# Two registers for the row bound of all indirect gathers, set once, in a sparse four-layer graph kernel

## The chip, the cores and the metric

The kernel runs on one core of a Trainium2 chip. The metric is device time in microseconds for the whole launch, as the median of several runs. Lower is better.

## What is computed

Four graph layers follow each other on the same node features and the same adjacency matrix: 8 batches, 2048 nodes, 128 features. The adjacency matrix is random, symmetric, with about 17 neighbours for each node. Layers 0 and 2 are attention with 8 heads of 16, masked by the adjacency, followed by a feed-forward part:

```python
scores = jnp.einsum('bnhd,bmhd->bhnm', Q, K) / jnp.sqrt(HEAD_DIM)
scores = jnp.where(mask, -jnp.inf, scores)
attn = jax.nn.softmax(scores, axis=-1)
attn_out = jnp.einsum('bhnm,bmhd->bnhd', attn, V).reshape(B, N, OUT_DIM)
x = _layer_norm(h + (attn_out @ Wo + bo), ln1_g, ln1_b)
y = jax.nn.relu(x @ W1 + b1) @ W2 + b2
x = _layer_norm(x + y, ln2_g, ln2_b)
```

Layers 1 and 3 are graph attention with one score for each edge:

```python
h = x @ W
e = (h @ a_src)[:, :, None] + (h @ a_dst)[:, None, :]
e = jnp.where(e >= 0, e, NEG_SLOPE * e)
att = jax.nn.softmax(jnp.where(adj[None] == 0, -jnp.inf, e), axis=-1)
y = jnp.einsum('bij,bjd->bid', att, h) + x          # then a layer norm
```

## The kernel before

The kernel works on the edges that exist and not on the full 2048 x 2048 matrix. It first reads the adjacency matrix in 16 blocks of 128 rows and makes, for each of 32 units of 64 nodes, a list of neighbour indices: the tile `idx`, 128 partitions by 32 units by 9 columns (`TILES`), so 9 columns of 128 edge slots for each unit and, as two groups of 32 nodes share a step, 5 steps (`TG`) for each unit. Beside the lists it makes matrices of ones and zeros (`hot`, kept in DRAM as `hots`) that spread a node's query to its edge slots and add the slots' results up again on TensorE (PE).

A layer first has a table in DRAM with one row for each node, made by the layer before (`project`, L1533 and L1535; the rows leave SBUF through `trows`). For attention a row holds keys and values of all 8 batches (2048 f32), for graph attention 1040 f32. Then for each unit and step `gather` (L1654 and after) issues one or two indirect DMAs on GpSimd (POOL): each reads one column of `idx` and fetches 128 rows of the table into a buffer `kv`, of which there are six. 9 such DMAs for each unit, 32 units and 4 layers make 1152.

An attention step then goes: PE spreads the queries (`qe`, L1734), VectorE (DVE) multiplies them with the gathered keys (L1746) and sums each head (L1753), ScalarE (ACT) takes the exponential (L1763), POOL multiplies it into the values (L1772; DVE does it for some steps), and PE adds the slots up (L1804). A graph attention step has DVE add and fold the scores (L1970, L1977, L1992), ACT the exponential (L1982), and PE add up (L2008). After the five steps of a unit follow the normalizations, the feed-forward part and the rows of the next table.

The order of all this is made before the launch: every piece of work has a key and estimated costs, a planner (`Plan.order`) simulates the engines with these and writes one fixed order for each engine. So each engine takes its instructions strictly in that order. POOL's queue holds, in the layers, almost only two kinds of work: the gathers (L1671) and the multiplications (L1772). Ahead of both stand semaphore waits where the order of the engines needs them.

An indirect DMA is given a bound for its row index. Rows above it are left out without an error (`oob_is_err=False`); the empty edge slots of a list use that. The bound is `nodes - 1`, where `nodes` is 2048, or 1920 for the first steps of the first four units, which read a table whose last rows are still missing: 128 of the 1152 gathers. The DMA instruction takes the bound from a register of POOL. With `bounds_check` given as a number, the language puts a register move ahead of each gather, on POOL's queue.

Where the profile names POOLq, it is POOL's sequencer, which takes the instructions in order, performs moves and semaphore waits itself and hands the rest to the engine.

Of the kernel before, what the change touches and what calls it, by code (L numbers as in the profile page):

```python
# [20 lines left out]
P = 128  # L21
# [50 lines left out]
class Dense:  # L72
# [10 lines left out]
    def __init__(self, ctx, tc, x, adj, w, out):  # L83
        self.tc, self.nc, self.w, self.x_in, self.out = tc, tc.nc, w, x, out
        self.B, self.N, _ = x.shape
        self.NB = self.N // P
        self.NC = self.N // CH

        def pool(name, **kw):
            return ctx.enter_context(tc.tile_pool(name=name, **kw))  # L90

        self.const = pool("const", bufs=1)
        self.dram = pool("dram", bufs=1, space=DRAM)
        self.dram2 = pool("dram2", bufs=2, space=DRAM)
        self.ps_s = pool("ps_s", bufs=2, space=PSUM)
        self.ps_acc = pool("ps_acc", bufs=1, space=PSUM)
        self.ps_m = pool("ps_m", bufs=1, space=PSUM)

        self.constants()
        self.layers = [  # L100
            self.mha_weights(n) if kind is MHA else self.gat_weights(n)
            for n, kind in enumerate(LAYERS)
        ]
        self.masks(adj)

        self.one = pool("one", bufs=1)
        self.two = pool("two", bufs=2)
        self.three = pool("three", bufs=3)
        self.four = pool("four", bufs=4)
        self.kpool = pool("kpool", bufs=9)  # L110
        self.vpool = pool("vpool", bufs=5)
        self.turn = 0
# [656 lines left out]
class Sparse:  # L769
# [15 lines left out]
    def __init__(self, ctx, tc, x, xt, xk, adj, w, out):  # L785
        self.tc, self.nc, self.w, self.xt_in, self.xk_in, self.out = tc, tc.nc, w, xt, xk, out
        self.B, self.N, _ = x.shape
        self.NB = self.N // P
        self.NU = self.N // UNIT
        self.HB = self.B // 2  # L790

        def pool(name, **kw):
            return ctx.enter_context(tc.tile_pool(name=name, **kw))

        self.nc.scalar.preload_act_table_set("natural_log_exp_and_others")
        self.const = pool("const", bufs=1)
        self.dram = pool("dram", bufs=1, space=DRAM)
        self.plan = Plan(self.nc)
        self.op, self.cell = self.plan.op, self.plan.cell
        for tag, bufs in SBUF_BUFS.items():  # L800
            self.plan.pool(tag, pool(f"sb_{tag}", bufs=bufs), bufs, tag in BY_KEY)
        for tag, bufs in PSUM_BUFS.items():
            self.plan.pool(tag, pool(f"ps_{tag}", bufs=bufs, space=PSUM), bufs)

        self.constants()
        self.weights_at = [Cell() for _ in LAYERS]
        self.keys_at = Cell()
        self.late = self.tight = False
        self.whole()
        self.gates = {}  # L810

        self.gate = self.keys_at
        keys = self.const.tile([P, 2 * P], F32, name="Wkv_0")
        self.fill(0, (keys[:, 0:P], w[0]["Wk"]), (keys[:, P : 2 * P], w[0]["Wv"]), at=self.keys_at)
        self.layers = [{"Wkv": keys}]


        self.tables = [
            self.dram.tile([self.N, self.B * (2 * P if kind is MHA else P + 2)], F32, name=f"table_{n}")
            for n, kind in enumerate(LAYERS)  # L820
        ]
        self.table = [Cell() for _ in LAYERS]
        self.rest = [Cell() for _ in LAYERS]

        self.xd = self.dram.tile([self.NU, P, CH], F32, name="xd")
        self.x_at = [Cell() for _ in range(self.NU)]
        self.hots = self.dram.tile([self.NU, P, HOT], F8, name="hots")
        self.hots_at = [Cell() for _ in range(self.NU)]
        self.kept = {}
        self.ends_at = [None] * self.NU  # L830
        self.t = self.const.tile([P, self.NU, P // GROUP * self.HB], F32, name="t")
        self.t_at = [Cell() for _ in range(self.NU)]
        self.idx = self.const.tile([P, self.NU, TILES], I32, name="idx")
        self.idx_at = [Cell() for _ in range(self.NU)]


        self.owner = self.const.tile([P, self.NU, TG, 2], F32, name="owner")
        self.ends = self.const.tile([P, self.NU, 2], F32, name="ends")
        self.late_ends = self.const.tile([P, LATE, 2], F32, name="late_ends")
        self.shift = self.const.tile([P, LATE, 2], F16, name="shift")  # L840

        self.empty = self.const.tile([P, self.NU, TILES], F32, name="empty")


        self.seen = self.const.tile([P, 4, self.NB], F32, name="seen")
        self.stats = self.const.tile([P, 6], F32, name="stats")
        self.eps = self.fixed("eps", EPS)
        self.half = self.fixed("half", 0.5)
        self.rows_n = self.fixed("rows_n", float(self.N))
        self.huge = self.fixed("huge", 1e30)  # L850

# [590 lines left out]
    def rows(self, tag, shape, axis, unit, name=None):  # L1444

        if self.made is None:
            return self.cell(tag, shape, name=name)
        if self.taken == len(self.made):
            self.made.append(self.cell(tag, shape, name=name))
        cut = (slice(None),) * axis + (slice(self.blocks.start * unit, self.blocks.stop * unit),)  # L1450
        self.taken += 1
        return Part(self.made[self.taken - 1], lambda t: t[cut])
# [210 lines left out]
    def gather(self, n, u, t, width, key, kv, rows, writes, shares=()):  # L1663

        tiles = 1 if t == TG - 1 else 2
        nodes = self.N - P if u < LATE and t < PAIRS else self.N

        def start(e):
            for j in range(tiles):
                col = 2 * t + j  # L1670
                e.indirect_dma_start(  # L1671
                    out=rows(kv.tile, j),
                    out_offset=None,
                    in_=self.tables[n][0:nodes],
                    in_offset=bass.IndirectOffsetOnAxis(ap=self.idx[:, u, col : col + 1], axis=0),
                    bounds_check=nodes - 1,
                    oob_is_err=False,
                )

        self.op(  # L1680
            {"POOL": 1.3 * tiles},
            start,
            key,
            reads=[*self.sources(n, u, t), self.idx_at[u]],
            writes=writes,
            shares=shares,
            port="wait",
            dma=120 * tiles * width * 4,
        )
# [539 lines left out]
```

## Time and profile before

| what | value |
|---|---|
| median of 3 runs | 2952.3 us (2948.37, 2952.3, 2961.27) |
| the profiled execution, its own time | 2960.0 us |
| its span, first to last instruction | 2958.3 us |
| granted TensorE clock, mean over the span | 0.893 |
| PE, DVE, ACT, POOL busy | 77%, 78%, 48%, 72% |
| DMA traffic | 1022.52 MB, 346 GB/s on average |

The profile is of one execution. "Busy" is the share of the span in which an engine's own work ran; instructions that a sequencer performs itself, such as register moves and waits, are not in it. A group's row gives the line, the engine, the operation, what it writes and reads, how often, its total and mean time, and how long the engine stood idle just ahead of it, with what ended most of that idle time; "issue" is idle time that the profile can put down to no wait. The row of slices under DMA gives the busy share of the DMA engines in tenths, for 40 equal parts of the span.

### The profile page before, as it was taken

The numbers are of one execution on the slowest core, as the hardware profiler recorded it, in microseconds if no ns is written. First come the engines' busy times: TensorE is split into PE (matmuls) and PEld (weight loads), VectorE is DVE, ScalarE is ACT, GpSimd is POOL, SyncE is SP. The second block draws the span as 40 slices with busy tenths as digits, with TensorE's granted clock in tenths as the row PEclk, the third lists the DMA queues.
The fourth block names the chain that finished last, engine by engine and source line by source line (L and its number), as shares of the span: only waits on it lengthen the run. The fifth ranks groups of instructions, "written<-read, shape, count | busy, mean of one in ns | idle before, by whom it ended". The sixth has DMA issues, their size and how long they took to land. (4 is left out here: it accounts for less than half of the span.)

```text
span 2958.3 us, 59482 instructions
## 1 busy us (share of the span) xinstructions
PE 2282.4 (77%) x21668; PEld 1334.4 (45%) x21668; DVE 2305.8 (78%) x3785; ACT 1423.9 (48%) x4899; POOL 2137.4 (72%) x1455
## 2 busy tenths in 40 slices
PE   6567778777887777778877688888888888777775
PEld 4423333333333334666665243343433333566664
DVE  7789999898977787555554888888898898576665
ACT  5535555555544443555554244444444444354443
POOL 1287778778878775666663788778887786677774
PEclk8778989989989999889898799999999999887787
DMA  8788889889879887999998898988998997899996
GB/s 302 274 315 333 336 324 341 320 330 369 332 299 353 313 308 267 362 410 410 405 406 325 321 380 333 376 339 347 368 374 338 357 370 278 328 404 407 404 398 268
DMA packets 248062, 1022.52 MB, mean 346 GB/s; under 512 B 39184, under 2 KB 52880, under 8 KB 175856
## 3 DMA queue, kind: packets, MB, share of 16 engines
q0 software_dynamic: 166464, 864.44, 75.4%
q1 hardware_dynamic: 81296, 154.18, 14.1%
q8 instruction: 174, 2.85, 0.4%
q14 instruction: 128, 1.05, 0.1%
HBM read 978.23 MB, written 88.08 MB: 360 GB/s over the span
## 5 line engine op out<-in xcount | busy, mean ns | idle before, releaser
L1671 POOL DMA_INDIRECT kv<-table,idx x1152 | 1199.7, 1041 | 583.2 <-issue 324.7
L1772 POOL TENSOR_TENSOR kv<-kv 128x2048 f32<-128x2048 f32 (+1 forms) x259 | 924.6, 3581 | 95.5 <-ACT kv L1763 91.2
L1746 DVE TENSOR_TENSOR kv<-qe,kv 128x2048 f32<-128x2048 f32 (+1 forms) x320 | 662.2, 2069 | 120.6 <-DMA kv<-table,idx 65.1
L1753 DVE TENSOR_REDUCE s<-kv 128x128 f32<-128x2048 f32 (+1 forms) x320 | 659.6, 2061 | 9.9
L1734 PE MATMUL qe<-q_sb,hot 32*128 32x512 f32 (+1 forms) x2304 | 398.2, 697 | 180.4 <-DVE kv L1746 176.6
L1804 PE MATMUL acc<-kv,hot 128*32 128x512 f32 (+1 forms) x2304 | 370.8, 654 | 71.8 <-POOL kv L1772 44.5
L2008 PE MATMUL acc_q<-kv,w 128*32 128x129 f32 (+1 forms) x4608 | 206.8, 311 | 119.6 <-DVE w L1992 98.7
L1992 DVE TENSOR_TENSOR w<-hot,e 128x512 f32<-128x512 f32 (+1 forms) x384 | 221.4, 598 | 53.2 <-ACT e L1982 37.3
L1763 ACT ACTIVATE kv<-s 128x128 f32<-128x128 f32 (+1 forms) x320 | 95.3, 298 | 347.6 <-DVE s L1753 222.7
L1734 PEld LDWEIGHTS qe<-q_sb,hot 32*128 32x128 f32 (+1 forms) x2304 | 106.8, 197 | 310.3 <-DVE kv L1746 251.4
L2008 PEld LDWEIGHTS acc_q<-kv,w 128*32 128x32 f32 (+1 forms) x4608 | 162.6, 128 | 149.7 <-DVE w L1992 110.6
L1970 DVE TENSOR_TENSOR e<-te,kv 128x16 f32<-128x16 f32 (+1 forms) x320 | 58.5, 183 | 195.7 <-DMA kv<-table,idx 194.5
L1607 ACT ACTIVATE junk<-ps_c 128x128 f32<-128x128 f32 x494 | 136.6, 277 | 137.8 <-PE ps_c L1495 117.3
L1471 ACT COPY trows<-ps_p 128x512 f32<-128x512 f32 (+1 forms) x238 | 112.8, 475 | 178.2 <-PE ps_p L1535 100.0
L1804 PEld LDWEIGHTS sums<-kv,hot 128*32 128x32 f32 (+1 forms) x2304 | 90.6, 120 | 212.0 <-issue 206.9
L1495 PE MATMUL ps_c<-centre,r 128*128 128x128 f32 x1024 | 153.7, 298 | 31.6 <-DVE r L1881 17.3
L1505 PE MATMUL ps_f<-x,W 128*128 128x512 f32 (+1 forms) x264 | 153.2, 666 | 29.0 <-ACT hidden L1901 21.7
L1982 ACT ACTIVATE e<-e 128x16 f32<-128x16 f32 (+1 forms) x320 | 65.0, 212 | 228.5 <-DVE e L1977 221.2
L1495 PEld LDWEIGHTS ps_c<-centre,r 128*128 128x128 f32 x1024 | 133.1, 203 | 73.1 <-DVE r L1881 32.2
L1804 PEld LDWEIGHTS acc<-kv,hot 128*32 128x32 f32 (+1 forms) x2304 | 55.9, 115 | 217.5 <-POOL kv L1772 107.6
L1911 PE MATMUL ps_y<-hidden,W 128*128 128x512 f32 (+1 forms) x264 | 146.6, 644 | 8.6 <-ACT hidden L1901 7.3
L1640 ACT ACTIVATE normed<-ps_c,rstd 128x128 f32<-128x128 f32 x495 | 143.2, 370 | 5.7 <-DVE normed L1642 3.8
(204 smaller groups left out, 3850.7 us busy)
## 6 DMA issues: line engine op xcount, KB each, us to landing
x<-xd SPq DMA_DIRECT2D x96, 256.0 KB
xd<-xnew SPq DMA_DIRECT2D x93, 256.0 KB
kv<-table,idx POOLq DMA_INDIRECT x1152
table<-trows SPq DMA_DIRECT2D x128, 130.0 KB
kv<-adj_dram SPq DMA_DIRECT2D x16, 1024.0 KB
table<-trows SPq DMA_DIRECT2D x32, 512.0 KB
table<-trows SPq DMA_DIRECT2D x64, 256.0 KB
kv<-xk_dram SPq DMA_DIRECT2D x8, 1024.0 KB
```

The costliest lines, as they stand in the source:

```text
L1495: e.matmul(ps.tile[:, cols], lhsT=flat(x.tile)[:, cols], rhs=self.centre, start=True, stop=True)
L1505: lambda e: e.matmul(ps.tile, lhsT=w, rhs=x.tile, start=True, stop=True),
L1640: e.activation(out, in_, AF.Copy, scale=by)
L1671: e.indirect_dma_start(out=rows(kv.tile, j), out_offset=None, in_=self.tables[n][0:nodes], in_offset=bass.IndirectOffsetOnAxis(ap=self.idx ...
L1734: e.matmul(qe.tile[:, j, hf, :], lhsT=hot.tile[rows, t * P : (t + 1) * P], rhs=q.tile[rows, :], start=True, stop=True,)
L1746: e.tensor_tensor(k, qe.tile[:, 0:tiles].rearrange("p j h c -> p (j h) c"), k, ALU.mult)
L1753: e.tensor_reduce(s.tile[:, 0 : tiles * heads].rearrange("p (q c) -> p q c", q=2 * tiles), k, axis=mybir.AxisListType.X, op=ALU.add,)
L1772: e.tensor_tensor(v, v, w.unsqueeze(3).to_broadcast([P, 2 * tiles, heads // 2, HD]), ALU.mult)
L1804: e.matmul(out[rows, :], lhsT=hot.tile[:, col : col + GROUP * (3 - tiles)], rhs=rhs[:, 2 * j + hf, :], start=(t == 0), stop=(t == TG - 1),)
L1911: lambda e, f=f, ps=ps: e.matmul(ps.tile, lhsT=L["W2"][:, f, :], rhs=hidden.tile[:, f, :], start=(f == 0), stop=(f == FFN // P - 1),),
L1992: e.tensor_tensor(w.tile[:, :, j : j + tiles, :].rearrange("p x j c -> p j x c"), oh[:, j : j + tiles].unsqueeze(2).to_broadcast(shape), e ...
L2008: e.matmul(acc(b)[at : at + GROUP * (3 - tiles), :], lhsT=w.tile[:, hf * hb + b, j : j + 3 - tiles, :].rearrange("p j c -> p (j c)"), rhs= ...
```

## The change

Two registers of POOL are taken in the setup and set once, one to 1919 and one to 2047. Each gather names the one that fits its table rows, instead of a number.

```diff
         self.half = self.fixed("half", 0.5)
         self.rows_n = self.fixed("rows_n", float(self.N))
         self.huge = self.fixed("huge", 1e30)
+        self.bounds = {}
+        for nodes in (self.N - P, self.N):
+            self.bounds[nodes] = self.nc.gpsimd.alloc_register(f"last_{nodes}")
+            self.nc.gpsimd.reg_mov(self.bounds[nodes], nodes - 1)
...
                     in_=self.tables[n][0:nodes],
                     in_offset=bass.IndirectOffsetOnAxis(ap=self.idx[:, u, col : col + 1], axis=0),
-                    bounds_check=nodes - 1,
+                    bounds_check=self.bounds[nodes],
                     oob_is_err=False,
                 )
```

## The prediction, made before the changed kernel was run

> **What bounds the kernel now.** I read the page first, from its busy table to its DMA queues and its chain, then the rows of the gather line, then POOL's timeline at one ordinary place. The page:
>
> ```profile
> span 2958.3 us, 59482 instructions
> ...
> PE 2282.4 (77%) x21668; PEld 1334.4 (45%) x21668; DVE 2305.8 (78%) x3785; ACT 1423.9 (48%) x4899; POOL 2137.4 (72%) x1455
> ...
> DMA  8788889889879887999998898988998997899996
> ...
> q0 software_dynamic: 166464, 864.44, 75.4%
> q1 hardware_dynamic: 81296, 154.18, 14.1%
> q8 instruction: 174, 2.85, 0.4%
> ...
> DMA 7%; PE 7%; DVE 5%; issue 4%; ACT 1%; POOL 1%; POOLq 0%; DVEq 0%; SPq 0%; ACTq 0%
> ...
> L1671 POOL DMA_INDIRECT kv<-table,idx x1152 | 1199.7, 1041 | 583.2 <-issue 324.7
> ```
>
> The reader is to see three things. The 16 DMA engines are busy for 75.4 + 14.1 = 89.5% of the span, and the gathers (the software queue) are five sixths of that, so what paces the kernel first is how fast gathered rows land. DVE, PE and POOL follow at 72 to 78%. And the chain that ended last spends 7% of the span on gathers' landings, 1% on POOL and 0% on POOLq, which is POOL's sequencer: the place where the instruction lives that is removed here. The one number that could tempt is the last: 583.2 us of POOL idle ahead of gathers, 324.7 us of it marked "issue", that is, no wait that the profile shows. The question is whether the register moves fill that idle time.
>
> The answer for the gather's line names the moves, on POOL's queue:
>
> ```profile
> L1671 POOLq MOVE  x1152: 29/29/29, 122.2 to 2922.6; - x192
> L1671 POOL DMA_INDIRECT kv<-table,idx x1152: 984/992/3095, 129.1 to 2927.7; - x192
> L1671 POOLq EVENT_SEMAPHORE  x551: 17/42/25638, 122.3 to 2919.9; - x184
> ```
>
> and POOL's timeline shows an ordinary run of gathers:
>
> ```profile
> 1000.57 3.69 POOL L1772 TENSOR_TENSOR kv<-kv 128x2048 f32<-128x2048 f32 x1
> 1004.42 1.02 POOL L1671 DMA_INDIRECT kv<-table,idx  x1 [0.16 <-POOL kv L1772]
> 1005.75 0.99 POOL L1671 DMA_INDIRECT kv<-table,idx  x1 [0.31 <-issue]
> 1007.05 0.99 POOL L1671 DMA_INDIRECT kv<-table,idx  x1 [0.30 <-issue]
> 1008.35 0.99 POOL L1671 DMA_INDIRECT kv<-table,idx  x1 [0.30 <-issue]
> 1010.00 0.98 POOL L1671 DMA_INDIRECT kv<-table,idx  x1 [0.67 <-issue]
> ```
>
> The two gathers that start between 1007.0 and 1009.7 us have no move between them: asked for that stretch, the gather's line answers
>
> ```profile
> L1671 POOL DMA_INDIRECT kv<-table,idx x2: 987/988/990, 1007.1 to 1008.3; - x2
> L1671 POOLq EVENT_SEMAPHORE  x1: 3222/3222/3222, 1006.1 to 1006.1; - x1
> ```
>
> and yet the gap is the same 0.30 us as where a move ran (one starts at 1005.9). So the gap of 0.30 us belongs to the gather, not to the move. The 0.67 us at 1010.00 is the other kind: here the sequencer had been held by a wait for a semaphore (3.222 us from 1006.08, so until 1009.30) and needed 0.70 us from its end to the gather's start. The move of that gather had run at 1005.94, ahead of the wait.
>
> **The change, part by part.**
>
> *Removed: 1152 moves on POOL's queue, one ahead of each gather; added: two, once, in the setup.* In the built program nothing else differs: the order on every engine, the waits and their values, the addresses are the same; the 1024 gathers from all 2048 rows name another register. By the row the moves are 1152 x 29 ns = 33.4 us of recorded time. What one occupies of the sequencer is more: where a semaphore instruction follows a move, it starts 75 ns after the move's start in 168 of the cases (1005.943 and 1006.018 for instance). 1150 x 75 ns = 86 us is therefore the most that can go, if every slot were on the path.
>
> *How much of it is on the path.* I went through POOL's records in the program's order, gather by gather.
> - 849 gathers start 0.30 us after the end of a gather, and 132 some 0.16 us after the end of a multiplication (L1772): 981 of 1152 start as soon as POOL itself lets them. The start-to-start time of two gathers is 1295 ns in the median with no move, one move or two inside it (248, 358 and 47 pairs). The sequencer is faster than that: move, gather, move is 516 ns from start to start. It runs ahead and then stands behind the full queue; taking 75 ns out of 516 leaves it standing longer. Price nothing; the cover is the 1295 ns of the gather in front.
> - In 698 cases the move stands directly ahead of its gather. The least time from the end of such a move to the gather's start is 1.17 us, where a gather that the sequencer alone holds back needs 0.70 us. None of the 698 waits for its move. Price nothing, with 0.47 us of cover in the worst of them.
> - In 454 cases one or more semaphore instructions stand between the move and the gather. 110 gathers start about 0.70 us after such an instruction ends, so the sequencer does set their start. But in every one of the 110 the semaphore instructions had waited, 0.74 us at the least, longer than the 75 ns by which the wait would now begin earlier. The wait ends when another engine or a landing ends it; beginning it earlier moves nothing. Price nothing.
> - The other idle time ahead of gathers waits for something named: landings of earlier gathers 58.1 us, PE's sums 52.9 us. No move in it.
>
> *The two moves in the setup.* They stand behind the constants, where POOL has to wait anyway: 111.1 us of POOL's idle time ahead of the first stores of `hots` waits for ACT. 2 x 75 ns = 0.15 us under that cover. Price nothing.
>
> *Instruction fetch.* POOL's program shrinks from 510,784 to 437,184 bytes, most of it for these moves. 73,600 bytes at the 346 GB/s of the DMA row are 0.2 us of DMA time; both instruction queues together take 0.5% of the engines. Bounds 0 and 0.2 us; I take 0.
>
> Weighed against a page: the 29 ns are the row. The Trainium skill, "Perfetto Trace Analysis", section on sequencer-only instructions, says that the profile reports of these only the execution, and that fetch, decode and push stay hidden. The trace agrees in that the slot is 75 ns and not 29; by the row alone the upper end would be 33 us, by the page's reading it is the larger figure. And one that speaks against the change: the skill's "DMA: Bandwidth & Descriptors", section on the anatomy of one DMA, gives the sequencer's dispatch an estimate of about 50 ns of a fixed 2 us that is mostly the write's receipt, so by it saving on the issue side is worth nothing. The trace has a far dearer dispatch, 0.70 us from the end of a wait to the start; the sum is zero by both, for the reason above.
>
> *The sum.* 0 us, against the profiled execution's own 2960.0 us. That one is 7.7 us over the median of the three runs (2952.3 us, from 2948.37 to 2961.27), which is within their spread. So I predict 2952 us.
>
> **What a measurement can tell.** The three runs lie within 12.9 us of each other, 0.44%; I take 0.5%, or 14.8 us, as what can be told from no change: faster is under 2937.5 us, slower over 2967.1 us.
>
> **The rivals.**
>
> *A: some of the moves are on the path after all.* For it: 324.7 us of idle time marked "issue" ahead of gathers, and POOL at 72% busy plus 849 gaps of 0.30 us (255 us, another 9%), which makes POOL nearly an owner of the time in the attention layers. If the sequencer's slots counted in full, 86 us go: 2952 - 86 = 2866 us. If only the 110 gathers count that the sequencer holds back, 110 x 75 ns = 8 us: 2944 us, which is not told from no change. For a gain that can be seen, 14.8 us / 75 ns = 197 moves must be on the path. Against it: the list above finds none, and the DMA engines, at 89.5%, would take much of what POOL gains. A middle value, a third of the slots, is 2923 us.
>
> *B: slower, by gathers that come between SP's loads and their users.* If the sequencer hands on gathers earlier, their packets stand ahead of loads that SP issues at that time. The place is the load of the one-hot matrices, `hot<-hots`, 61 of them in the attention layers; the chain has one of them, 10.21 us long at 2323.10 us. A gather there is 128 rows of 2048 f32, 1.05 MB, or 3.0 us at 346 GB/s. One gather ahead of a load delays it by that; from five loads on the chain on (5 x 3.0 = 15 us) it shows. With ten it is 2952 + 30 = 2982 us. Against it: a gather starts earlier only where its move held it back, which the rows don't show.
>
> *C: the change does not do what it says*, if the moves came back at each gather in the built program. They don't: 1154 moves become 4 on POOL, setup included. The time would be that of the forecast anyway, so it has no price of its own.
>
> **How the numbers follow.** No visible change, between 2938 and 2967 us: 0.72. Within it the spread of the runs alone gives 2945 to 2961 us. Rival A with a gain that can be seen: 0.18, because the bounds between 0 and 86 us rest on starts that I ordered by inference, and a sequencer can hold an engine back in ways that no record shows; its likely part is the lower half of the gain, down to about 2923 us. Rival B or another shift of the traffic: 0.10. The range that leaves out 2 in 10 or less reaches from 2923 us (a third of the slots) to 2970 us (one step of 3.0 us past the threshold for slower). Faster 0.18, within 0.5% 0.72, slower 0.10.
>
> **What would show it.** The gather line keeps its 1152 gathers at a median of about 992 ns, and the gap between two of them stays 0.30 us; the line has no MOVE any more; POOL's idle time ahead of gathers stays near 583 us, marked "issue" near 325 us; the software queue stays near 75% with the same 864.44 MB. If the gap between gathers falls to about 0.23 us, the move was in it, and A holds. If gathers that follow a wait start 0.62 us after it instead of 0.70 us, the register's write was still in their way. If the idle time ahead of `hot<-hots` users grows, it is B. A time that moves by over 0.5% with all these unchanged would make the working wrong in a way that none of my rows shows.

## The result and the profile after

The change moves nothing that can be measured. The changed kernel takes 2959.76 us (median of 20 runs, 2945.77 to 2974.17), the kernel before 2956.93 us (20 runs beside them, 2945.85 to 2971.18). The ratio is 1.0008, with a 95% interval of 0.9993 to 1.0024. The prediction was no visible change, 2952 us, with a range from 2923 to 2970 us.

The page of the changed kernel, its head, DMA queues, chain and gather row:

```profile
span 2960.2 us, 58332 instructions
...
PE 2278.8 (77%) x21668; PEld 1334.1 (45%) x21668; DVE 2305.1 (78%) x3785; ACT 1420.9 (48%) x4899; POOL 2140.5 (72%) x1455
...
q0 software_dynamic: 166464, 864.44, 75.3%
...
DMA 6%; DVE 6%; PE 6%; issue 3%; POOL 2%; ACT 2%; SPq 0%; DVEq 0%; POOLq 0%; ACTq 0%
...
L1675 POOL DMA_INDIRECT kv<-table,idx x1152 | 1202.6, 1044 | 583.6 <-issue 331.4
```

The program has 58332 instructions instead of 59482: the 1150 moves that went. Everything else stands where it stood: the engines' busy time, the queue of gathers, and POOL's idle time ahead of gathers, 583.6 us against 583.2 us, the time that could have tempted one to expect a gain. The shares of the chain (the work that ended last, followed back from the last instruction) are less of a witness: it could be followed back only to 2186 us (2184 us in the kernel before), so they speak for the last 26% of the span. The gather's line (L1675 now) no longer has a MOVE, and its gathers have the same median of 992 ns:

```profile
L1675 POOL DMA_INDIRECT kv<-table,idx x1152: 984/992/3088, 130.5 to 2928.6; - x192
L1675 POOLq EVENT_SEMAPHORE  x551: 17/42/25938, 123.6 to 2920.0; - x184
```

POOL's timeline of the changed kernel, at about the same place as before:

```profile
1008.12 1.02 POOL L1675 DMA_INDIRECT kv<-table,idx  x1 [0.16 <-POOL kv L1776]
1009.45 0.99 POOL L1675 DMA_INDIRECT kv<-table,idx  x1 [0.30 <-issue]
1010.75 0.99 POOL L1675 DMA_INDIRECT kv<-table,idx  x1 [0.30 <-issue]
1012.04 0.99 POOL L1675 DMA_INDIRECT kv<-table,idx  x1 [0.30 <-issue]
```

The gap between two gathers is still 0.30 us, and after a multiplication 0.16 us. So the gap never held the move.

What did get shorter is the sequencer's own work. Where one semaphore instruction, two gathers and another semaphore instruction follow each other, the time from the end of the first to the start of the last is 957 or 958 ns in the changed kernel (127 places) and 1075 to 1082 ns in the kernel before, with the two moves (70 places). With one gather in between it is 500 ns. A move therefore occupied the sequencer for 59 to 62 ns (59 is used below), and a gather costs it some 458 ns. All moves together were 1150 x 59 ns = 68 us of sequencer time (72 us by the larger figure). That all of it had lain beside the gathers is what the experiments are to show.

### The profile page after: what moved, and what is told of

Same layout as the page of the kernel before. It is cut to its first block, busy times and chain, and to the rows that moved or that the text cites. A ratio compares the mean times of both kernels' runs of the same rounds, so it can differ in the third digit from the quotient of the medians.

```text
span 2960.2 us, 58332 instructions
## 1 busy us (share of the span) xinstructions
PE 2278.8 (77%) x21668; PEld 1334.1 (45%) x21668; DVE 2305.1 (78%) x3785; ACT 1420.9 (48%) x4899; POOL 2140.5 (72%) x1455
## 5 line engine op out<-in xcount | busy, mean ns | idle before, releaser
L1675 POOL DMA_INDIRECT kv<-table,idx x1152 | 1202.6, 1044 | 583.6 <-issue 331.4
L2012 PE MATMUL acc<-kv,w 128*32 128x129 f32 (+1 forms) x2304 | 116.2, 302 | 48.0 <-DVE w L1996 37.5
```

The source lines that it names most:

```text
L1675: e.indirect_dma_start(out=rows(kv.tile, j), out_offset=None, in_=self.tables[n][0:nodes], in_offset=bass.IndirectOffsetOnAxis(ap=self.idx ...
L2012: e.matmul(acc(b)[at : at + GROUP * (3 - tiles), :], lhsT=w.tile[:, hf * hb + b, j : j + 3 - tiles, :].rearrange("p j c -> p (j c)"), rhs= ...
```

## The experiments

Theory: POOL's sequencer needs about half a microsecond for a gather and its engine 1295 ns, so the sequencer runs ahead and register work is free until it fills the difference, (1295 - 458) / 60 = some 14 operations for each gather. Rival: the sequencer's slots are on the path, and what the change gained was given back elsewhere (to the DMA, say). To tell them apart, register work is added to the changed kernel, in growing numbers. A second question is what time on POOL's engine itself would have been worth.

**Moves to a spare register.** The edit, with 8, 16 or 32 in the loop:

```diff
+                for _ in range(8):
+                    self.nc.gpsimd.reg_mov(self.spare, nodes - 1)
                 e.indirect_dma_start(
```

> The changed kernel with 8 moves to a spare register ahead of each gather, 9216 in all. Two gathers with nothing else between two waits take POOL's sequencer 957 ns in the changed kernel, and 1075 ns with two moves in the kernel before, so a move is 59 ns and a gather some 458 ns. Theory (the moves run under the cover of the gather in front, which takes POOL's engine 1295 ns): 458 + 8 x 59 = 930 ns is still under 1295 ns, so nothing moves: 2957 us, within 0.5%; the gap between two gathers stays 0.30 us. Rival (the slots are on the path and the change's gain was given back elsewhere): 8 x 1152 x 59 ns = 544 us more at the full share, 181 us at a third.

> The same with 16 moves for each gather. Theory: 458 + 16 x 59 = 1402 ns is 107 ns over what a gather takes of POOL's engine, so the cover ends here: at most 849 x 107 ns = 91 us of POOL time, of which a part is on the path; 0 to 60 us more. Rival with a share for every slot: twice what 8 moves cost, 1088 us at the full share, 363 us at a third.

> The same with 32 moves for each gather. Theory: 458 + 32 x 59 = 2346 ns for a gather, 1051 ns over the cover; the two graph attention layers, with 288 gathers each and few multiplications between them, then need 676 us each for the gathers alone, against some 500 us now: 200 to 800 us more, most of it in these layers, and the gap between two gathers grows from 0.30 to about 1.35 us. Rival with a share for every slot: four times what 8 moves cost.

Measured: 2953.81, 2954.50 and 2953.64 us, ratios 0.9989 (0.9970 to 1.0008), 0.9991 (0.9972 to 1.0009) and 0.9984 (0.9963 to 1.0005). These three say nothing on the question. Nothing reads the spare register, and the moves are not in the built program: each of the three traces has 58332 instructions, as the changed kernel's has, and none on the line of the moves. The three are the changed kernel three times more, 30 runs of it, whose three medians lie within 0.2% of the kernel before.

**Register work that the gather depends on.** So that it can't be left out, the bound itself is changed and changed back; here with 8 operations, and with longer lists for 12, 16 and 32:

```diff
+                b = self.bounds[nodes]
+                for k in (1, 3):
+                    self.nc.gpsimd.reg_add(b, b, k)
+                    self.nc.gpsimd.reg_alu(b, b, 4096 * k, ALU.bitwise_xor)
+                for k in (3, 1):
+                    self.nc.gpsimd.reg_alu(b, b, 4096 * k, ALU.bitwise_xor)
+                    self.nc.gpsimd.reg_sub(b, b, k)
                 e.indirect_dma_start(
```

> The changed kernel with 8 register operations ahead of each gather that the gather's bound depends on (add and exclusive-or, and back, so that the bound comes out the same): 9216 in all, on POOL's sequencer alone. Taken at a move's 59 ns each, a gather needs 458 + 8 x 59 = 930 ns of the sequencer. Theory (under the cover of the 1295 ns that a gather takes of POOL's engine): nothing moves, within 0.5% of 2957 us; the gap between two gathers stays 0.30 us. Rival (slots are on the path, and the change's gain was given back elsewhere): 544 us more at the full share, 181 us at a third; 207 us at the share of 0.38 that the memset on POOL's engine showed (86 us more for some 226 us).

> The same with 16 register operations for each gather. Theory at 59 ns each: 458 + 16 x 59 = 1402 ns, 107 ns over the cover; at most 849 x 107 ns = 91 us of POOL time, at the memset's share of 0.38 35 us more: 2957 to 2992 us. If an operation takes longer than 59 ns, the cover ends sooner and the cost is larger; the gap between two gathers then shows it. Rival: twice what 8 operations cost.

> The same with 32 register operations for each gather. Theory at 59 ns each: 458 + 32 x 59 = 2346 ns for a gather, 1051 ns over the cover. The two graph attention layers, with 288 gathers each and no multiplications on POOL, then need 676 us each for the gathers alone, against some 500 us now; the gap between two gathers grows from 0.30 to about 1.35 us: 200 to 800 us more, most of it in these layers. Rival: four times what 8 operations cost, no threshold.

These three ran on another chip of the same kind, on which the kernel before took 3180.79 us, 7.6% more than on the first. There they gave 3247.67, 3151.34 and 3776.74 us: ratios 1.0209 (1.0171 to 1.0246), 0.9899 (0.9863 to 0.9935) and 1.1863 (1.1819 to 1.1908). Slower with 8, faster with 16 and far slower with 32 is what neither theory had expected of the first two. The layers tell where it comes from: from the first gather of a layer to that of the next, the two attention layers took 1019 and 912 us with 8 operations, near the 1012 and 904 us of the changed kernel on the first chip, but the two graph attention layers 590 and 592 us against 470 and 443 us. Packets of 4160 bytes, the graph attention rows, took 190 ns on average there, and 167 ns on the first chip; packets of 8192 bytes took the same 340 ns. With 16 operations the graph attention layers took 535 and 530 us.

With 8 operations it is not the traffic that holds these two layers up on that chip. The DMA engines are busy for 87% and 80% of them there, and for 98% and 94% with the same program on a chip like the first (run below). PE is what is late, as the chain and the gathers' idle time on the slower chip say (this chain reaches back over 76% of the span):

```profile
PE 29%; issue 13%; DVE 13%; DMA 8%; another core or an unknown queue 4%; ACT 4%; POOL 4%; POOLq 1%; SPq 0%; DVEq 0%; ACTq 0%
...
L1682 POOL DMA_INDIRECT kv<-table,idx x1152 | 1188.3, 1032 | 870.0 <-issue 365.0 <-PE sums L2019 155.3 <-PE acc_q L2019 119.2
```

The matmuls that add up the slots (L2019) follow each other there with pauses: from the start of one to the next it is 0.3 to 0.8 us in 141 and 187 places of the two layers, against 9 and 10 on the chip like the first, and the steps sum to 298 and 385 us against 191 and 255 us. That is 107 and 129 us, most of what the layers took longer (121 and 145 us). With 16 operations there were 82 and 99 such pauses. What makes PE pause on that chip, and less often with 16 operations, was not found, and the kernel before has no trace from there.

The two that were in question were therefore run again, with the changed kernel beside them, and the chip was like the first (the kernel before: 2955.34 us):

> The changed kernel again, beside the same kernels as before, because the chip of the last three runs gave the kernel before 3181 us instead of 2956 us, with graph attention layers that took longer. Whatever the chip, the changed kernel stands within 0.5% of the kernel before.

> The kernel with 8 register operations ahead of each gather again. One was 62.5 ns from start to start, so a gather needs 458 + 8 x 62.5 = 958 ns of POOL's sequencer, under the 1295 ns of its engine. Theory (hidden): within 0.5% of the changed kernel on the same chip. If the 2.1% of the first time were the operations' own, it comes back: some 60 us more on any chip.

> The kernel with 16 register operations again: 458 + 16 x 62.5 = 1458 ns for a gather, 163 ns over what its engine takes. Theory: the attention layers, whose packets went at the same pace on both chips, take some 13 and 24 us more, as they did; the graph attention layers, 288 x 1458 ns = 420 us against the 467 us that they take on the chip of the first comparison, little more: 35 to 70 us more there. If the 1.0% less of the first time were the operations' own, it comes back: 30 us less on any chip.

Measured: the changed kernel 2957.29 us, ratio 1.0011 (0.9990 to 1.0033); 8 operations 2955.18 us, ratio 1.0003 (0.9982 to 1.0025); 16 operations 3007.00 us, ratio 1.0174 (1.0145 to 1.0203), 52 us more than the kernel before. This is what the theory gave: nothing for 9216 register operations, and a cost once they fill the difference. With 8, the line of the additions and POOL's timeline show the work and no trace of it on the engine:

```profile
L1677 POOLq ALU_OP  x2304: 35/35/45, 121.9 to 2911.4; - x192
```

```profile
1009.31 1.02 POOL L1682 DMA_INDIRECT kv<-table,idx  x1 [0.49 <-PE ps_t L1486]
1010.63 0.99 POOL L1682 DMA_INDIRECT kv<-table,idx  x1 [0.30 <-issue]
1011.93 0.99 POOL L1682 DMA_INDIRECT kv<-table,idx  x1 [0.30 <-issue]
```

With 16, the gap between gathers is 0.47 us in the median, as POOL's timeline shows in a graph attention layer. The chain, which here reaches back over 27% of the span, has 3% on POOL's sequencer and names the operations:

```profile
1300.41 0.99 POOL L1682 DMA_INDIRECT kv<-table,idx  x1 [0.47 <-issue]
1302.18 0.99 POOL L1682 DMA_INDIRECT kv<-table,idx  x1 [0.78 <-issue]
1303.64 0.99 POOL L1682 DMA_INDIRECT kv<-table,idx  x1 [0.47 <-issue]
```

```profile
issue 8%; DVE 5%; PE 4%; DMA 4%; POOLq 3%; ACT 1%; POOL 1%; DVEq 0%; SPq 0%; ACTq 0%
DMA kv<-table,idx 4%; DVE kv L1757 2%; DVE s L1764 1%; POOLq L1678 1%; POOLq L1681 1%; POOLq L1680 1%; PE qe L1745 1%; PE acc_q L2019 1%; POOLq L1677 1%; DVE w L2003 1%; PE ps_c L1499 1%; PE ps_te L2042 0%; ACT junk L1611 0%; POOL kv L1682 0%; PE ps_y L1922 0%
```

0.99 + 0.47 = 1.46 us from start to start is the sequencer's 458 + 16 x 62.5 = 1458 ns. It is the gap that tells 16 operations from 8, not the chain: with 8 the chain names POOL's sequencer too (2%, reaching back over 74% of the span), at an unchanged time and an unchanged gap:

```profile
DMA 25%; PE 16%; DVE 14%; issue 10%; POOL 4%; ACT 3%; POOLq 2%; SPq 0%; DVEq 0%; ACTq 0%
```

The split by layers was not as expected. Nearly all of the cost, 20 and 35 us, is in the graph attention layers, within the 35 to 70 us put on them; but the 13 and 24 us put on the attention layers did not come (1005 and 907 us against 1004 and 903 us of the changed kernel beside it). A likely reason, not tested, is that POOL's multiplications in those layers let the sequencer get ahead again.

The changed kernel is thus within 0.5% of the kernel before each time that both ran on a chip like the first. Its expectation says "whatever the chip"; on a slower one it was not run.

**Both sides of the threshold.**

> 12 register operations ahead of each gather: 458 + 12 x 62.5 = 1208 ns of the sequencer for a gather, still under the 1295 ns of its engine; 16 of them (1458 ns) were over it and took 51 us more. Theory (a threshold at 13 operations): within 0.5% of the kernel before, and the gap between two gathers stays 0.30 us. Rival (the cost grows with the number, and 8 were lost in the spread): 12/16 of 51 us, 38 us more.

> 32 register operations again, for the other side of the threshold: 458 + 32 x 62.5 = 2458 ns for a gather. Theory: the sequencer then paces the graph attention layers, 288 x 2458 ns = 708 us of issue for each, and some 65 us around it, as in the run on the slower chip (774 us each), whatever the chip's DMA does; with attention layers of some 1090 and 1000 us and 129 us of lists 3770 us, the same time as on the slower chip, 27% over the kernel before. If the chip's DMA still counted, the time is lower, by up to the 225 us that separate the kernel before on the two chips.

These came to another slow chip (the kernel before: 3203.82 us). 32 operations gave 3788.47 us, 1.1805 (1.1751 to 1.1858): the 3770 us of the expectation, and the 3776.74 us of the other slow chip, within 0.5%. POOL's timeline in a graph attention layer shows the sequencer setting the pace, 2.46 us from start to start where 458 + 32 x 62.5 = 2458 ns was reckoned, and the chain has its largest parts in "issue" and on POOLq:

```profile
1305.05 0.99 POOL L1682 DMA_INDIRECT kv<-table,idx  x1 [1.47 <-issue]
1307.51 0.99 POOL L1682 DMA_INDIRECT kv<-table,idx  x1 [1.47 <-issue]
1309.97 0.99 POOL L1682 DMA_INDIRECT kv<-table,idx  x1 [1.47 <-issue]
```

```profile
issue 38%; POOLq 25%; PE 13%; POOL 10%; DMA 6%; DVE 6%; ACT 2%; SPq 0%; DVEq 0%; another core or an unknown queue 0%; ACTq 0%
```

That this time is the same on any chip was not shown, since both runs came to slow ones.

12 operations gave 3230.77 us, ratio 1.0089 (1.0063 to 1.0116): 27 us more, a miss for "within 0.5%", and less than the rival's 38 us. The gap between two gathers is 0.30 us still in the median, but in some 630 places; with 8 operations it was so in some 750 on the other slow chip, and in some 830 on the chip like the first. One cause can be read from the trace in part: the sequencer pauses now and then between two register operations of one gather, some 580 times here, by 0.5 us on average, and a pause comes on top of the 1208 ns. On the chip like the first the pauses are fewer and shorter, 61 with 8 operations, of 0.30 us, against some 200 of 0.50 us for the same program on the slow chip. The sum of the long ones overstates the time lost, as the records behind many of them stand closer together than 62.5 ns. PE's matmuls pause on this chip too, in 160 and 178 places of the two graph attention layers. What part of the 27 us either makes was not measured, and with slow chips on one of which 8 operations cost 2.1% and 16 gain 1.0%, this is no place to find a threshold. So the threshold is bracketed by 8 and 16 on chips like the first, and not closer.

**Time on POOL's engine.** One small piece of work for the engine, in place of register work:

```diff
+                self.nc.gpsimd.memset(self.spare, 0.0)
                 e.indirect_dma_start(
```

> The changed kernel with one memset of 128x256 f32 to a spare tile on POOL ahead of each gather: engine time instead of sequencer time. From the rows (128x128: 204 ns, 128x16: 123 ns) one takes about 0.30 us, and the gap ahead of a gather changes from 0.30 us to 0.02 + 0.16 us, so 0.18 us more for each gather, 207 us of POOL time. If landings of gathered rows pace the kernel, 0 to 60 us more; if POOL's engine does, about 200 us more. It tells what a saving on POOL's engine could have been worth.

Measured on a chip like the first: 3041.44 us, ratio 1.0278 (1.0243 to 1.0314), 86 us more. The chain of this kernel:

```profile
POOL 29%; DMA 15%; PE 12%; DVE 9%; issue 6%; ACT 2%; POOLq 0%; SPq 0%; DVEq 0%; ACTq 0%
```

It reaches back over 75% of the span. That of the changed kernel's second profile reaches over 74%, so the two can be compared, and POOL has 6% there:

```profile
DMA 24%; PE 19%; DVE 15%; issue 7%; POOL 6%; ACT 3%; DVEq 0%; SPq 0%; POOLq 0%; ACTq 0%
```

The timeline with the memset:

```profile
1019.07 1.00 POOL L1677 DMA_INDIRECT kv<-table,idx  x1 [0.16 <-issue]
1020.05 0.34 POOL L1676 MEMSET spare<- 128x256 f32 x1
1020.55 1.00 POOL L1677 DMA_INDIRECT kv<-table,idx  x1 [0.16 <-issue]
```

From gather to gather it is 1.49 us now instead of 1295 ns, and after a multiplication 0.48 us until the gather instead of 0.16 us: 849 x 0.195 + 175 x 0.32 = 222 us more of POOL's time by this estimate, of which 86 us, 0.39, reach the end. So POOL's engine is not idle capacity: its time counts, in part. Its sequencer's time does not, as long as it is hidden. Where it is not, it counts like the engine's: with 16 operations 849 x 0.163 = 138 us more, of which 52 us, 0.37, reach the end. (What the memset costs other engines, by writing to SBUF, is in the 86 us too and was not measured by itself; DVE's busy time did not grow, 2303.8 us against 2305.1 us.)

## Why the prediction was right, step by step

- *"The gap of 0.30 us belongs to the gather, not to the move."* Right: it is 0.30 us with no move, with one and with 8 register operations. With 16 operations, where the sequencer needs longer than the engine, it is 0.47 us.
- *"1150 x 75 ns = 86 us is the most that can go."* Mis-sized. 75 ns was read from the start of a move to the start of the semaphore instruction behind it. The difference that taking it away makes is 59 to 62 ns, so the upper end was 68 to 72 us. The forecast did not rest on it, but rival A's prices did, and its third of the slots was some 2929 us rather than 2923 us.
- *"981 of 1152 start as soon as POOL itself lets them", "None of the 698 waits for its move", "In every one of the 110 the semaphore instructions had waited".* Right as to the sum, which was zero. The first is shown by the dose: nothing for 8 operations, 52 us for 16. The other two were not tested by themselves. The third agrees with the count: 110 to 120 gathers start about 0.70 us after a semaphore instruction ends, in the changed kernel as in the kernel before.
- *"If gathers that follow a wait start 0.62 us after it instead of 0.70 us, the register's write was still in their way."* It was not: the gathers that the sequencer holds back start 0.70 us after it at the least, in both.
- *"What paces the kernel first is how fast gathered rows land."* Too strong. The memset shows that time on POOL's engine counts at 0.39, so several limits take turns. It did no harm, since the moves were on neither. Had they been on the engine, 68 us would have been worth some 26 us by that share, 0.9%, and would have been seen.
- *"0% on POOLq".* Read from a chain that covers the last 26% of the span and not all of it. The changed kernel's second profile, whose chain covers 74%, has 0% there too, so the reading holds for those layers.
- *Instruction fetch, "Bounds 0 and 0.2 us; I take 0".* Priced by DMA time alone, while the sequencer pauses too: 0.30 us for every 128 instructions of POOL (last section), so by estimate 9 pauses for the 1150 moves, 2.7 us of the sequencer. The sum did not need it, as no time of the sequencer came out at the end.
- *Rival A* falls: rather than 197 moves on the path, there is room for some 8 operations more at every gather. *Rival B* has nothing to stand on: POOL's idle time ahead of gathers is unchanged, and ACT waits for `hot<-hots` 91.2 us in all against 87.5 us before. *Rival C* was excluded beforehand.
- *The sum against the profiled run's own time:* 2960.0 us for the one and 2962.0 us for the other, 2 to 3 us over the medians of the 20 runs. Of the 7.8 us between 2952 us and the measured 2959.76 us, 4.6 us are the start: the three runs had a median of 2952.3 us, the 20 have 2956.93 us. The rest is within the interval.

## What to carry to other kernels

Here an instruction that the sequencer performs itself cost nothing as long as the engine behind it needed longer for its work than the sequencer for its list. Compare the two paces first (516 ns with a move, and 1295 ns), and only then add up instructions. Idle time marked "issue" ahead of a DMA is not by itself time that fewer instructions give back: look whether the gap is the same where those instructions are missing. To measure whether a resource matters, add to it in steps, and look in the trace whether the work is there: the moves whose result nothing read were not. Look also how far back a chain reaches before its shares are compared.

## What was not expected

Chips of the same kind differ by 7.6 and 8.4% on the kernel before (2956 us against 3181 and 3204 us), and on one of the slower two register work went either way by 1 to 2%. The gap ahead of a gather is 0.30 us behind a gather and 0.16 us behind a multiplication or a memset on POOL.

A register operation on POOL's sequencer takes 62.5 ns from start to start, with a pause of 0.30 us now and then: 61 times in 9216 operations and 136 times in 18432 on the chip like the first. These pauses keep step with the program. Counted along POOL's records, every one of the 136 stands at the same place of a block of 128 instructions, to within 8, and so do 59 of the 61. One of the two instruction queues of the DMA (q14) has 191 and 263 packets in these two runs and 119 in the changed kernel's, 72 and 144 more, one for every 128 operations; for the 1150 moves that went it is 9 packets (128 before). So the pauses go with the loading of the program. The longer ones on the slow chips, 0.4 us and more, keep to no such place.
